# Cross-attention with a state-space tail: two chunk pairs' weighted values issued together in every second step

## The chip, the cores and the metric

The kernel runs on one core of one Trainium2 chip. The metric is the device time of one execution in microseconds (us), the median of several. A core has five engines that each take their own instructions in order and wait for one another through semaphores: TensorE (PE, matrix products into the accumulator memory PSUM; its weight loads are listed apart as PEld), VectorE (DVE), ScalarE (ACT), GpSimd (POOL) and SyncE (SP, which here only issues transfers).

## The reference

The input `x` is 4096 rows of 512, the context 3202 rows of 512. Both are layer-normalized with the same gain and shift, then eight attention heads of 64 go from `x` to the context; the result is projected and added to `x`. A second layer norm, a projection to 64 states, a scan along the 4096 rows (`s = silu(s @ A.T) + u`), and a projection back follow, with two more additions. The part around the change is the attention:

```python
scores = jnp.einsum('bhqd,bhkd->bhqk', q, k) * (1.0 / np.sqrt(HD))
attn = jax.nn.softmax(scores, axis=-1)
out = jnp.einsum('bhqk,bhkd->bhqd', attn, v)
```

Everything is float32. The scan comes last and is done in 16 interleaved chunks.

## The kernel before

**Three stages.** First the context is normalized, keys and values are computed and written to memory, and the first block of queries is made. Then the attention loop runs. Then the last rows are projected and the scan and the output follow. The change lies in the attention loop.

**The tiling of the loop.** The 4096 queries are eight blocks `Q` of 512. A *unit* is one block, one pair of heads `hp` (four of them) and one half of the block (256 queries): 64 units. The 3202 keys are 26 chunks of 123 or 124, taken as 13 pairs (`NDC = 13`), so a unit has 13 *steps* `c = 0..12`, and there are 832 steps. One step handles two heads x two chunks x 256 queries: a tile of 123 x 1024.

**What one step's tile goes through.**

- `scores` (L460): four float32 products on PE (two recorded passes each, so x8) into a PSUM tile `s`; there are two such tiles in turn (`ps_s`, `bufs=2`). They use the array as two row halves of 64. ACT then copies `s` to SBUF as `p` (L470).
- `running` (L481), one step later: DVE takes the running maximum `top` from `s`. The tile `s` is free again only after this and the copy.
- After the 13th step, `maximum`: PE transposes `top` (`tt`, L492), DVE reduces it (`m`, L499), PE spreads the result over the partitions (`mb`, L507). This takes three steps.
- `subtract` (L515): DVE takes `mb` off `p`, 16 steps (13 + `LAG`) after the scores.
- `weights` (L525), one step later: ACT takes the exponential; POOL adds it to `acc` (L534).
- `product` (L543), one further step later: four products on PE (x8) of `p` with the values into `po`, two column halves of 64.
- `finish` after a unit's last product: ACT copies `po` (L586), POOL folds `acc` (L589), PE transposes (`pd`, L595), DVE reduces and inverts (L600, L601), ACT widens (L603), PE transposes (`rb`, L608), DVE multiplies (L614).

**The order is written by hand.** `manual_schedule` keeps the order of the code on each engine. In a step at position `r` of its unit (`r` is the chunk pair whose scores are made) the loop issues: the running maximum of the step before, the exponential of an older one, scores, subtraction, product, then `mb` at r = 2, then *background* work, then `tt` at r = 0. The product lags the scores by 18 = 13 + 5 steps, so at position `r` it is that of chunk pair (r + 8) mod 13, of the unit before or the one before that: pair 8 at r = 0, 9 at r = 1, 12 at r = 4, 0 at r = 5.

**Background** is a queue of generators, advanced a little in each step: `finish` of every unit, `project` of a finished block (four tiles: the output projection `pa`, L628, on PE, then a layer norm and the state projection `pu`), and `queries` for the next block (transposes `tp_x` of four tiles, then four batches `pq`, L172). In a standard block the first and last units and most of the units of the last block have only `finish`; three units carry `project`, two carry the query transposes, one carries the four `pq` batches.

**Buffers.** `sp_` holds the tiles `p`: 20 of them. `ps_o` holds one `po`. K and V tiles of a head pair are 13 each (`kp`), loaded four steps ahead by SP.

Of the kernel before, what the change touches and what calls it, by code (L numbers as in the profile page):

```python
# [22 lines left out]
NDC = NCH // 2  # L23
# [5 lines left out]
LAG = 3  # L29
# [7 lines left out]
def keys(c):  # L37
    return CK if c < GC else CK - 1


def key0(c):
    return c * (CK - 1) + min(c, GC)
# [3 lines left out]
def xattn_ssm_kernel(  # L46
# [100 lines left out]
    def queries(Q):  # L147

        xns = []
        for half in range(2):  # L150
            xn = xnp.tile([P, NC, QU], F32, tag="xn", name=f"xn_{Q}_{half}")
            xns.append(xn)
            for t in range(NT // 2):
                r = Q * QB + half * QU + t * P
                xt = xp_.tile([P, H], F32, tag="x", name=f"x_{r}", bufs=3)
                nc.sync.dma_start(xt, x[r : r + P, :])
                yield False
                scaled = normalize(xt, P, f"x{r}", later=True)
                yield False
                yield False  # L160
                xh = scaled()
                yield False
                tp = transposes(ps_m, "m", xh, P, f"x{r}")
                yield True
                nc.scalar.copy(xn[:, :, t * P : (t + 1) * P], tp)
                yield False
                yield False
        for hp in range(NC):
            pq = ps_m.tile([P, 512], F32, tag="m", name=f"pq_{Q}_{hp}")
            for half in range(2):  # L170
                for i in range(NC):
                    nc.tensor.matmul(  # L172
                        pq[:, half * QU : (half + 1) * QU],
                        wq[:, i, hp * P : (hp + 1) * P],
                        xns[half][:, i, :],
                        start=(i == 0),
                        stop=(i == NC - 1),
                    )
            yield True
            t = qp.tile([P, QB], F32, tag="q", name=f"q_{Q}_{hp}")  # L180
            nc.scalar.activation(
                t, pq, AF.Identity, bias=bias[:, hp : hp + 1], scale=HD**-0.5
            )
            qt[Q, hp] = t
            yield False
# [179 lines left out]
    with tc.manual_schedule():  # L365
# [17 lines left out]
        for c in range(NCH):  # L383
# [28 lines left out]
            for hp in range(NC):  # L412
# [13 lines left out]
                for b in range(g * GC, c + 1, 2):  # L426
                    m, k = 2 * keys(b), key0(b) - key0(g * GC)
# [6 lines left out]
    lctx = ExitStack()  # L434
# [11 lines left out]
    op = actx.enter_context(tc.tile_pool(name="op", bufs=6))  # L446
    small = actx.enter_context(tc.tile_pool(name="small", bufs=2))
    kp = lctx.enter_context(tc.tile_pool(name="kp", bufs=NDC))
    sp_ = lctx.enter_context(tc.tile_pool(name="sp_", bufs=NDC + LAG + 4))

    o_t = {}

# [19 lines left out]
    def running(w, c):  # L472

        n, s = keys(2 * c), w["ps"]
        if c == 0:
            w["top"] = w["s"][0]
            return
        before = w["top"]
        if c == 1:
            w["top"] = accp.tile([CK, 2, 2, QU], F32, tag="top", name=f"top_{w['name']}")  # L480
        nc.vector.tensor_tensor(w["top"][:n], s[:n], before[:n], ALU.max)  # L481
# [31 lines left out]
    def subtract(w, c):  # L513
        n, t = keys(2 * c), w["s"][c]
        nc.vector.tensor_tensor(  # L515
            t[:n],
            t[:n],
            w["mb"][:n].unsqueeze(2).to_broadcast([n, 2, 2, QU]),
            ALU.subtract,
        )  # L520

    def weights(w, c):

        n, t = keys(2 * c), w["s"][c]
        nc.scalar.activation(t[:n], t[:n], AF.Exp)  # L525
        if w["last"] and c in PE_SUMS:
            return
        before = w.get("acc")
        if before is None:
            w["acc"] = t  # L530
            return
        if c == 1:
            w["acc"] = accp.tile([CK, 2, 2, QU], F32, tag="acc", name=f"acc_{w['name']}")
        nc.gpsimd.tensor_tensor(w["acc"][:n], t[:n], before[:n], ALU.add)  # L534

    def product(w, c):

        n, t = keys(2 * c), w["s"].pop(c)
        if c == 0:
            w["po"] = ps_o.tile([P, 2, QU], F32, tag="o", name=f"po_{w['name']}")  # L540
        for b in range(2):
            for a in range(2):
                nc.tensor.matmul(  # L543
                    w["po"][a * HD : (a + 1) * HD, 0, :],
                    vts[(*w["at"][:2], c)][:n, b, a * HD : (a + 1) * HD],
                    t[:n, a, b, :],
                    start=(c == 0 and b == 0),
                    stop=(c == NDC - 1 and b == 1),
                )
        if w["last"] and c in PE_SUMS:  # L550

            if c == PE_SUMS[0]:
                w["pd"] = ps_m.tile([P, 512], F32, tag="m", name=f"pd_{w['name']}")
            sums(w["pd"], t, n, c == PE_SUMS[0], False)

    def sums(pd, t, n, start, stop):
        for b in range(2):
            for a in range(2):
                nc.tensor.matmul(
                    pd[a * HD : (a + 1) * HD, :QU],  # L560
                    ones[:n],
                    t[:n, a, b, :],
                    start=(start and b == 0),
                    stop=(stop and b == 1),
                )
# [109 lines left out]
    def load_k(i, c):  # L675

        Q, hp, half = units[i]
        if half == 0:
            t = kp.tile([P, 2 * CK], F32, tag="k", name=f"k_{Q}_{hp}_{c}")
            n = 2 * keys(2 * c)  # L680
            nc.sync.dma_start(t[:, :n], kd[hp, c, :, :n])
            kts[Q, hp, c] = t

    def load_v(i, c):
        Q, hp, half = units[i]
        if half == 0:
            t = kp.tile([CK, 2, P], F32, tag="v", name=f"v_{Q}_{hp}_{c}")
            n = keys(2 * c)
            nc.sync.dma_start(t[:n], vd[hp, c, :n])
            vts[Q, hp, c] = t  # L690
# [9 lines left out]
    def at(k):  # L700

        if 0 <= k < len(steps):
            return ws[steps[k][0]], steps[k][1]
# [15 lines left out]
    with tc.manual_schedule():  # L719
        for g in range(AHEAD):  # L720
            load_k(*steps[g])
        for g in range(len(steps) + NDC + LAG + 2):
            b = g - NDC - LAG
            if g + AHEAD < len(steps):
                load_k(*steps[g + AHEAD])
            if 0 <= b + AHEAD < len(steps):
                load_v(*steps[b + AHEAD])
            if g < len(steps):
                i, c = steps[g]
                Q, hp, half = units[i]  # L730
                if c == 0:
                    ws[i] = dict(
                        name=f"{Q}_{hp}_{half}", at=units[i], s={}, last=i == len(units) - 1,
                        q=qt[Q, hp][:, half * QU : (half + 1) * QU],
                    )
                    if (hp, half) == (1, 1) and Q + 1 < NQB:
                        rest.append(queries(Q + 1))
            now, prev, sub, exp, mul = at(g), at(g - 1), at(b), at(b - 1), at(b - 2)

            ends = {k: at(g - k)[0] for k in (1, 2, 3) if at(g - k) and at(g - k)[1] == NDC - 1}  # L740
            if 3 in ends and sub:
                subtract(*sub)
            if prev:
                running(*prev)
            if exp:
                weights(*exp)
            if now:
                scores(*now)
            if 3 not in ends and sub:
                subtract(*sub)  # L750
            if 2 in ends:
                next(ends[2]["max"])
            if mul:
                product(*mul)
                if mul[0]["last"] and mul[1] == NDC - 1:
                    finish_last(mul[0])
                elif mul[1] == NDC - 1:
                    first.append(finish(mul[0]))
                    if mul[0]["at"][1:] == (NC - 1, 1):
                        rest.insert(0, project(mul[0]["at"][0]))  # L760
            if 3 in ends:
                next(ends[3]["max"], None)
            background(more=1 not in ends)
            if 1 in ends:
                ends[1]["max"] = maximum(ends[1])
                next(ends[1]["max"])
        while first or rest:
            background()
# [200 lines left out]
```

## Time and profile before

| | before |
|---|---|
| median of 3 runs | 2682.13 us (2678.46 to 2682.83) |
| the profiled execution's own time | 2679.33 us |
| its span in the profile | 2677.4 us |
| PE, DVE, ACT, POOL busy, share of the span | 94%, 80%, 69%, 77% |
| mean granted TensorE clock | 0.977 of full |
| attention loop, first scores to last product | 304.8 to about 2538 us |

The profile is of one execution. Its page gives busy shares, the chain of work that ended last, groups of instructions by source line, and issues of transfers; the trace behind it answers for single stretches of time. In the listings of instructions in order of time the columns are the start in us, the duration in us, the engine, the line, the operation, the tile written <- the tiles read, their shapes, the count, and in brackets idle time before it and what ended it. The end of a product on PE is modelled, so the distance from one block's start to the next is the better measure. The table by stretches lists, for each engine, busy us and (x instructions), then the granted clock.

### The profile page before, as it was taken

How to read it: one execution, taken by the hardware profiler on the slowest of the kernel's cores; microseconds unless marked ns; L12 is line 12 of the kernel's file. 1: busy time of each engine (PE TensorE's matmuls, PEld its weight loads, DVE VectorE, ACT ScalarE, POOL GpSimd, SP SyncE). 2: the span in 40 equal slices, each digit the busy share in tenths (PEclk: the TensorE clock that was granted, in tenths of full speed). 3: DMA queues.
4: the chain of work that ended last, by engine and by line, in shares of the span. 5: the costliest groups of instructions: out<-in, count | busy, mean ns of one | idle time of the engine just before them, and what ended most of it. 6: DMA issues, size and time to landing. Idle time of an engine off the chain costs nothing.

```text
span 2677.4 us, 44182 instructions
## 1 busy us (share of the span) xinstructions
PE 2507.3 (94%) x16588; PEld 1424.4 (53%) x16588; DVE 2146.1 (80%) x2321; ACT 1836.0 (69%) x2085; POOL 2065.1 (77%) x1170
## 2 busy tenths in 40 slices
PE   7788799999999999999999999999999999999957
PEld 3333555555565556555555556555555565555533
DVE  2121298899979998999989897999799979999825
ACT  2122387787878787877878787878687878788610
POOL 1111099899979998999979897999799979999870
PEclk9889999999999999999999999999999999999976
DMA  4332221112212221122111221212112211221043
GB/s 123 90 92 85 77 67 45 46 57 68 70 41 58 59 75 47 53 67 70 58 50 56 81 60 43 61 52 82 33 55 69 69 42 58 58 65 54 27 147 126
DMA packets 167551, 176.62 MB, mean 66 GB/s; under 512 B 16701, under 2 KB 140645, under 8 KB 167335
## 3 DMA queue, kind: packets, MB, share of 16 engines
q1 hardware_dynamic: 155374, 158.21, 20.0%
q10 hardware_dynamic: 11961, 15.54, 1.9%
q8 instruction: 134, 2.20, 0.3%
q14 instruction: 82, 0.67, 0.1%
HBM read 143.81 MB, written 29.89 MB: 65 GB/s over the span
## 4 chain that ended last, share of the span: by engine, by line
PE 44%; DVE 26%; issue 18%; ACT 8%; POOL 3%; DMA 2%; SPq 0%; ACTq 0%; DVEq 0%; POOLq 0%
DVE top L481 17%; PE s L460 14%; PE po L543 12%; DVE p L515 5%; PE pq L172 4%; ACT p L470 4%; PE pa L628 4%; ACT p L525 2%; PE tt L492 2%; PE py_c L871 1%; DVE rd L600 1%; PE mb L507 1%; PE pu L660 1%; PE pk L415 1%; POOL acc L534 1%
## 5 line engine op out<-in xcount | busy, mean ns | idle before, releaser
L534 POOL TENSOR_TENSOR acc<-p,acc 123x1024 f32<-123x1024 f32 x698 | 1657.0, 2374 | 115.3 <-ACT p L525 73.8
L470 ACT COPY p<-s 123x1024 f32<-123x1024 f32 (+1 forms) x832 | 834.2, 1003 | 274.1 <-PE s L460 263.4
L515 DVE TENSOR_TENSOR p<-p,mb 123x1024 f32<-123x1024 f32 (+1 forms) x832 | 1001.2, 1211 | 0.8 <-PE mb L507 0.8
L460 PE MATMUL s<-q,k 64*123 64x256 f32 (+1 forms) x6656 | 940.0, 401 | 61.0 <-DVE top L481 50.6
L525 ACT ACTIVATE p<-p 123x1024 f32<-123x1024 f32 (+1 forms) x832 | 880.1, 1058 | 143.7 <-DVE p L515 137.1
L481 DVE TENSOR_TENSOR top<-s,top 123x1024 f32<-123x1024 f32 x704 | 856.7, 1217 | 139.4 <-ACT p L470 130.6
L543 PE MATMUL po<-p,v 123*64 123x256 f32 (+1 forms) x6656 | 901.3, 392 | 1.1 <-ACT o L586 0.9
L460 PEld LDWEIGHTS s<-q,k 64*123 64x123 f32 (+1 forms) x6656 | 559.3, 181 | 373.6 <-DVE top L481 172.5
L543 PEld LDWEIGHTS po<-p,v 123*64 123x64 f32 (+1 forms) x6656 | 404.8, 136 | 399.4 <-issue 223.1
L534 POOL TENSOR_TENSOR acc<-p,p 124x1024 f32<-124x1024 f32 x64 | 151.9, 2374 | 152.6 <-ACT p L525 152.3
L115 POOL TENSOR_SCALAR ve_c<-mv_c 123x1 f32<-123x1 f32 (+1 forms) x26 | 6.1, 233 | 187.7 <-DVE mv_c L113 181.6
L111 DVE BATCH_NORM_STATS2 st_c<-cx 123x6 f32<-123x512 f32 (+1 forms) x26 | 18.0, 692 | 151.8 <-DMA cx<-in_ctx_dram 151.8
L628 PE MATMUL pa<-wo,o 128*128 128x512 f32 x256 | 119.5, 611 | 2.3 <-DVE x L637 2.3
L172 PE MATMUL pq<-xn,wq 128*128 128x256 f32 x512 | 117.9, 383 | 0.0
L481 DVE TENSOR_TENSOR top<-s,p 124x1024 f32<-124x1024 f32 x64 | 77.9, 1217 | 40.6 <-DMA k<-kd 39.3
L125 ACT ACTIVATE xh_c<-cx,nmr_c,rstd_c 123x512 f32<-123x512 f32 (+1 forms) x26 | 21.1, 812 | 129.1 <-POOL nmr_c L119 129.1
L172 PEld LDWEIGHTS pq<-xn,wq 128*128 128x128 f32 x512 | 95.0, 190 | 20.7 <-issue 6.3
L415 PE MATMUL pk<-ct,wk 128*128 128x492 f32 (+2 forms) x224 | 99.0, 599 | 3.3 <-ACT ks L423 3.3
L390 PE MATMUL pv<-wv,ct 128*123 128x512 f32 (+1 forms) x208 | 96.3, 607 | 0.0
L589 POOL TENSOR_TENSOR both<-acc 124x512 f32<-124x512 f32 x63 | 80.8, 1283 | 4.9
L499 DVE TENSOR_REDUCE m<-tt 128x2 f32<-128x496 f32 x128 | 79.9, 665 | 0.7 <-PE tt L492 0.7
L628 PEld LDWEIGHTS pa<-wo,o 128*128 128x128 f32 x256 | 46.8, 192 | 62.2 <-issue 56.3
(157 smaller groups left out, 1335.3 us busy)
## 6 DMA issues: line engine op xcount, KB each, us to landing
k<-kd SPq DMA_DIRECT2D x352, 123.0 KB
v<-vd SPq DMA_DIRECT2D x352, 123.0 KB
x<-in_x_dram SPq DMA_DIRECT2D x32, 256.0 KB
xr<-in_x_dram SPq DMA_DIRECT2D x32, 256.0 KB
out_dram<-row_c ACTq DMA_DIRECT2D x32, 256.0 KB
k<-kd SPq DMA_DIRECT2D x64, 124.0 KB
v<-vd SPq DMA_DIRECT2D x64, 124.0 KB
x1d<-x SPq DMA_DIRECT2D x28, 256.0 KB
```

Source lines behind the costliest of these rows:

```text
L172: nc.tensor.matmul(pq[:, half * QU : (half + 1) * QU], wq[:, i, hp * P : (hp + 1) * P], xns[half][:, i, :], start=(i == 0), stop=(i == NC ...
L390: nc.tensor.matmul(pv[:n, :H], ct[:, i, o : o + n], wv[:, i, :], start=(i == 0), stop=(i == NC - 1),)
L415: nc.tensor.matmul(pk[:, :n_g], wk[:, i, hp * P : (hp + 1) * P], ct[:, i, :n_g], start=(i == 0), stop=(i == NC - 1),)
L460: nc.tensor.matmul(s[:n, a, b, :], kts[(*w["at"][:2], c)][r, b * n : (b + 1) * n], q[r], start=True, stop=True,)
L470: nc.scalar.copy(t[:n], s[:n])
L481: nc.vector.tensor_tensor(w["top"][:n], s[:n], before[:n], ALU.max)
L515: nc.vector.tensor_tensor(t[:n], t[:n], w["mb"][:n].unsqueeze(2).to_broadcast([n, 2, 2, QU]), ALU.subtract,)
L525: nc.scalar.activation(t[:n], t[:n], AF.Exp)
L534: nc.gpsimd.tensor_tensor(w["acc"][:n], t[:n], before[:n], ALU.add)
L543: nc.tensor.matmul(w["po"][a * HD : (a + 1) * HD, 0, :], vts[(*w["at"][:2], c)][:n, b, a * HD : (a + 1) * HD], t[:n, a, b, :], start=(c == ...
L589: nc.gpsimd.tensor_tensor(both, acc[:, :, 0, :], acc[:, :, 1, :], ALU.add)
L628: nc.tensor.matmul(pa, o_t[Q, c][:, t * P : (t + 1) * P], wo[:, c, :], start=(c == 0), stop=(c == NC - 1),)
```

## The change

The product of an even chunk pair is no longer issued in its own step. The step of an odd chunk pair issues two products, of the pair before and its own; the 13th chunk pair, which is even, is issued alone in its own step. Scores, subtraction, exponential, sums and background keep their places. Since an even tile `p` is read one step later, the pool `sp_` gets one more buffer, 21.

```diff
-    sp_ = lctx.enter_context(tc.tile_pool(name="sp_", bufs=NDC + LAG + 4))
+    sp_ = lctx.enter_context(tc.tile_pool(name="sp_", bufs=NDC + LAG + 5))
...
             if mul:
-                product(*mul)
+
+                u_, c = mul
+                for k in (c - 1, c) if c % 2 else (c,) if c == NDC - 1 else ():
+                    product(u_, k)
                 if mul[0]["last"] and mul[1] == NDC - 1:
                     finish_last(mul[0])
                 elif mul[1] == NDC - 1:
```

## The prediction

> **What bounds the kernel now.** I began with the page's busy shares and the chain that ended last.
>
> ```profile
> PE 2507.3 (94%) x16588; PEld 1424.4 (53%) x16588; DVE 2146.1 (80%) x2321; ACT 1836.0 (69%) x2085; POOL 2065.1 (77%) x1170
> PE 44%; DVE 26%; issue 18%; ACT 8%; POOL 3%; DMA 2%; SPq 0%; ACTq 0%; DVEq 0%; POOLq 0%
> ```
>
> PE looks like the bound, but both lines are means over different stages. So I cut one block's eight units apart, by their first score copy, and took the busy time of each engine in each: two with query transposes, one with `pq`, two with only `finish` ("plain"), three with `project`.
>
> ```profile
> 979.60:1012.30 32.70, 31.23 (x240) 17.84 (x236) 32.20 (x36) 27.87 (x33) 31.17 (x20) 1.00 0.11 36
> ...
> 1045.00:1090.10 45.10, 44.33 (x294) 28.79 (x294) 31.00 (x31) 28.55 (x34) 30.48 (x15) 1.00 0.07 21
> 1090.10:1121.00 30.90, 29.80 (x228) 16.86 (x228) 30.67 (x31) 26.12 (x28) 29.72 (x14) 1.00 0.28 78
> ...
> 1186.00:1224.90 38.90, 38.90 (x264) 21.45 (x261) 34.88 (x39) 28.18 (x32) 34.89 (x22) 1.00 0.18 53
> ```
>
> After the length come PE, PEld, DVE, ACT, POOL. The plain unit (third line) has DVE busy 30.67 of 30.90 us: DVE sets its length, PE does not. PE is the bound only with `project` (38.90 of 38.90) and in the `pq` unit. Of the 64 units 20 are plain, 14 have query transposes, 21 `project`, 7 `pq`, 2 are the lead-in.
>
> Next, the plain unit in order of time: PE from its position 0 to 3, DVE and ACT beside it.
>
> ```profile
> 1090.02 1.08 PE L543 MATMUL po<-p,v 123*64 123x256 f32 x8
> 1091.22 1.07 PE L492 MATMUL tt<-ident,top 124*128 124x124 f32 x8
> 1092.22 1.13 PE L460 MATMUL s<-q,k 64*124 64x256 f32 x8
> 1093.28 1.08 PE L543 MATMUL po<-p,v 123*64 123x256 f32 x8
> 1094.30 1.13 PE L460 MATMUL s<-q,k 64*123 64x256 f32 x8
> 1095.36 1.08 PE L543 MATMUL po<-p,v 123*64 123x256 f32 x8
> 1096.37 0.65 PE L507 MATMUL mb<-ident,m 128*124 128x128 f32 x4
> 1096.95 1.13 PE L460 MATMUL s<-q,k 64*123 64x256 f32 x8
> ```
>
> ```profile
> 1089.95 1.22 DVE L481 TENSOR_TENSOR top<-s,top 123x1024 f32<-123x1024 f32 x1
> ...
> 1095.64 1.22 DVE L481 TENSOR_TENSOR top<-s,p 124x1024 f32<-124x1024 f32 x1
> 1096.96 1.23 DVE L481 TENSOR_TENSOR top<-s,top 123x1024 f32<-123x1024 f32 x1
> ```
>
> ```profile
> 1095.53 1.02 ACT L470 COPY p<-s 123x1024 f32<-123x1024 f32 x1
> ...
> 1098.18 1.01 ACT L470 COPY p<-s 123x1024 f32<-123x1024 f32 x1 [0.69 <-PE s L460]
> ```
>
> Three readings. A block `s` followed by `po` takes 1.06 us (1092.22 to 1093.28), `po` followed by anything else 1.01. From the start of `s` to its copy is 1.23 us (1094.30 to 1095.53, 1096.95 to 1098.18), and the maximum can start 1.04 after the copy starts (elsewhere, 1054.05 to 1055.09): 2.27 in all. So the maximum over scores 2, issued at position 3 and started at 1096.96, could have started at 1094.30 + 2.27 = 1096.57: PE has 0.39 us in hand there, on a DVE that never rests.
>
> Last, blocks of one kind in a row: scores in the lead-in, products and sums (the same array split) in the tail.
>
> ```profile
> 329.53 2.00 PE L460 MATMUL s<-q,k 64*124 64x256 f32 x16
> 331.45 0.65 PE L507 MATMUL mb<-ident,m 128*124 128x128 f32 x4
> ```
>
> ```profile
> 2528.80 1.90 PE L543 MATMUL po<-p,v 123*64 123x256 f32 x16
> 2530.53 1.03 PE L559 MATMUL pd<-p,ones 123*64 123x256 f32 x8
> ```
>
> Two `s` and a switch take 1.92, so `s` after `s` costs 0.86; two `po` take 1.73, 0.87 each. A switch out of `s` thus costs 0.19-0.20, out of `po` 0.14-0.15.
>
> **What the Trainium skill says.** "TensorEngine Tiling (Array Packing)", Key Properties: changing the tiling mode, not just the tile, drains the array; agreed, with the two prices above. "TensorE: Matmul & The Clock Gate", The mechanism: products start and end in program order, so a second product delays the next scores; agreed, PE's blocks run in the order of the code. "PSUM — Partial Sum Buffer", PSUM bank collisions: the compiler adds a dependency between ACT and DVE on one bank, even for two reads; agreed, the maximum starts 1.04 us after the copy of the same `s`, never beside it. Same page, Engine vs sequencer instructions: DVE and ACT are strict first-in first-out, so a late maximum delays every subtraction behind it.
>
> **The change part by part.**
>
> *Array switches.* Where nothing else stands between, a pair of steps goes from four switches to two: 0.34 us of PE saved. Where the step without a product holds a `tt`, `mb` or other background, only 0.15. A plain unit has four pairs of the first sort and two of the second: 4 x 0.34 + 2 x 0.15 = 1.66 us. DVE covers PE there, so this buys nothing by itself.
>
> *Placement.* Pairs fall at r = 1 (chunk pairs 8, 9), 3, 6, 8, 10, 12; chunk pair 12 alone at 4; none at 0, 2, 5, 7, 9, 11.
>
> *Position 0, plain unit.* Before, product 8 ran from 1090.02 to 1091.03, and `tt` waited until 1091.22 for the maximum of 1089.95. Afterwards the pair at r = 12 pushes the scores of r = 0 from 1088.96 to 1089.64; `tt` could go at 1090.70, but still waits until 1091.22. Scores 1 start at 1092.22 as before. Product 8, formerly free, is now in front.
>
> *Position 1.* 1092.22 + 1.06 + 0.87 + 1.01 = 1095.16 for scores 2, against 1094.30: 0.86 late. Maximum at 1095.16 + 2.27 = 1097.43 instead of 1096.96: DVE stalls 0.47. Behind it wait the first subtraction, then the exponential on ACT, POOL's sum, the next maximum.
>
> *Position 2.* No product; `mb` at 1096.22, 0.15 early; scores 3 wait for the maximum that ends at 1096.86, start 1096.91.
>
> *Position 3.* Products 10, 11: scores 4 at 1096.91 + 2.94 = 1099.85 against 1099.03. Their maximum at 1102.12, while DVE (1101.50 before, + 0.47) is free at 1101.97: 0.15 more. The copy of `po` shifts with product 12 and pushes ACT some 0.05. Sum 0.65 us a plain unit, 20 of them: 13.0.
>
> *Later positions.* After a pair the next scores come 2.94 after the last, where DVE's pace is 2.26: 0.68 late. The scores of 1086.70 could be copied at 1087.93 and are at 1088.77, because an exponential stands before: 0.84 in hand covers it. With the cover gone it would be up to 0.68 at four places, 2.7 us a unit.
>
> *Query-transpose units.* DVE has a layer-norm statistic (0.69 + 0.18) just before that maximum; in the unit of 979.6 scores 2 at 984.12 feed a maximum at 987.11, 0.72 in hand; `tt` does not wait there, so scores 2 come only 0.57 late. At position 4 0.18 late on ACT remains: 0.2 x 14 = 2.8.
>
> *`pq` units.* PE runs without pause from scores 1 to scores 5: before 1047.09 to 1070.37. `tt` again waits for the maximum (1046.09), so product 8 moves into the stretch (+1.01) and two `po`-after-`po` save 0.14 each: +0.7 x 7 = 4.9.
>
> *`project` units.* I followed PE and DVE in the same way through 1152-1250, where PE bounds. Example, the unit of 1186: `tt` waits, so scores 1 start at 1188.64 (1188.66 before), then 1.06 + 0.87 + 1.01 + 3.65 for `pa`: scores 2 at 1195.23 against 1194.36, their maximum 0.86 later. Positions 2, 5, 7 and 9 have no product, but `mb`, `tp_y`, `pu`, `pa`: each loses 1.01 of PE work and gives it back, less 0.15 or 0.34, at the next position. DVE's lag falls to 0.1 by scores 5; the `pa` at position 9, with no product ahead of it, brings scores 10 at 1217.09 instead of 1217.56, and the maximum is 0.48 ahead; the next pair takes that back. It ends near +0.2: 7 blocks, 1.4.
>
> *Nothing:* the lead-in has no products. In the tail without scores the order on PE is the same. The later release of an even `p` is met by the 21st buffer (two steps between product and reuse, as before); V tiles are reloaded nine steps after their last product, eight afterwards; no DMA moves. No step adds an instruction.
>
> Sum 13.0 + 2.8 + 4.9 + 1.4 = 22 us. On the profiled execution's 2679.3 that is 2701; the median lies 2.8 above it, so **2704 us**, 0.8% slower.
>
> **Rivals.**
>
> 1. *PE's time counts everywhere* (the chain's 44% and 18% issue speak for it): 1.66 x 62 = 103 us saved, 2579. Against: DVE rests 0.23 us in a plain unit. 3 in 100.
> 2. *The other side, milder:* the 0.39 us in hand for scores 2 is really above 0.86 (were the copy able to start sooner after its scores, say), so nothing stalls in plain units, and in the 21 `project` units PE's saving of 1.09 us each (five pairs at 0.15, one at 0.34) is kept: -23 at best, so 2659 to 2682. It decides from the point where scores 2 are late by less than what is in hand. Against: 1.23 and 1.04 recur wherever the copy waits for PE. 5 in 100.
> 3. *Hidden:* the stalls for scores 2 and 4 are repaid by the gains with `project`: within 5 us. 7 in 100.
> 4. *The later positions are not covered:* 0.68 at one to two of the four pairs beyond position 4, on some 34 units: 22 + 23 to 46, so 2727-2750. For: `pd` (0.57) and `rb` (0.37) stand behind pairs at r = 6 and 8. Against: DVE's own reduction for them (0.67 + 0.18) falls there too. 17 in 100.
>
> The forecast itself has 68 in 100; its own range is 2694 to 2716: from 0.45 us a plain unit and nothing with `project` to 0.9 a plain unit and 0.4 on the others.
>
> **How the numbers follow.** 0.2% (5.4 us) is about what a measurement of this kernel can tell from no change. Faster: rivals 1 and 2, 0.07 (part of 2 falls within). Same: 0.08. Slower: 0.85. For 8 in 10 the range reaches from 2688, the lower part of the forecast, to 2728, the near edge of rival 4.
>
> **What would show it.** Right: in plain units, about 31.6 us instead of 30.9; the running maximum L481 waits on the copy about 0.47 for scores 2 in every plain unit, so its idle time (139.4 us now) grows by some 15-25 us; `po` x16 blocks of 1.9 us; PE busy down by up to 100 us; DVE busy unchanged. Wrong: plain units still 30.9 (the margin was larger), or shorter; stalls of L481 at positions 7, 9 or 11 (rival 4); a longer tail; or ACT or PE waiting for `p` buffers or V tiles.

## The result and the profile after

The changed kernel takes 2707.68 us (median of 6 runs, 2699.59 to 2713.03) against 2680.57 us for the kernel before (6 runs, 2675.43 to 2685.05): a ratio of 1.0097, 95% interval 1.0073 to 1.0121, so some 27 us slower. The profiled execution took 2711.29 us, its span is 2709.4 us.

From the page, the busy shares and the groups of the maximum and of the product:

```profile
PE 2461.1 (91%) x16588; PEld 1464.8 (54%) x16588; DVE 2148.3 (79%) x2321; ACT 1837.1 (68%) x2085; POOL 2066.3 (76%) x1170
...
L481 DVE TENSOR_TENSOR top<-s,top 123x1024 f32<-123x1024 f32 x704 | 856.3, 1216 | 169.6 <-ACT p L470 163.2
...
L543 PE MATMUL po<-p,v 123*64 123x256 f32 (+1 forms) x6656 | 822.2, 388 | 0.5 <-ACT o L586 0.5
```

TensorE did get its saving: it is 46 us less busy (2507.3 before), L543 alone 79 us less (901.3 before). DVE is as busy as before, 2148.3 against 2146.1, and idles 30 us more ahead of the running maximum L481 (139.4 before). The kernel got longer by about what DVE waits more.

The same units as before, cut at their first score copy (length, PE, PEld, DVE, ACT, POOL, then the granted clock): the second with query transposes, the one with `pq`, a plain one, the second with `project`.

```profile
1026.93:1060.81 33.88, 31.74 (x234) 19.00 (x235) 32.21 (x35) 28.55 (x33) 31.81 (x20) 0.95 0.28 83
1060.81:1106.46 45.65, 43.07 (x290) 29.32 (x290) 30.85 (x30) 28.41 (x33) 28.99 (x14) 1.00 0.06 19
1106.46:1138.02 31.56, 28.88 (x226) 17.43 (x226) 30.78 (x31) 26.20 (x30) 29.79 (x14) 1.00 0.29 80
...
1203.67:1242.36 38.69, 37.39 (x254) 21.66 (x254) 34.54 (x38) 28.03 (x32) 34.64 (x22) 1.00 0.19 54
```

The plain unit is 31.56 us instead of 30.93, with PE 0.9 us less busy. And the first line shows something else: a mean granted clock of 0.95 in the middle of the loop, where the loop ran at 1.00 throughout before.

PE through positions 0 to 4 of that plain unit, in order of time, and below it DVE's maxima over scores 1, 2 and 4 (parts left out) and ACT's copy of scores 2:

```profile
1106.65 1.07 PE L492 MATMUL tt<-ident,top 124*128 124x124 f32 x8 [0.46 <-DVE top L481]
1107.65 1.13 PE L460 MATMUL s<-q,k 64*124 64x256 f32 x8
1108.71 1.95 PE L543 MATMUL po<-p,v 123*64 123x256 f32 x16
1110.59 1.13 PE L460 MATMUL s<-q,k 64*123 64x256 f32 x8
1111.65 0.65 PE L507 MATMUL mb<-ident,m 128*124 128x128 f32 x4
1112.34 1.13 PE L460 MATMUL s<-q,k 64*123 64x256 f32 x8
1113.40 1.95 PE L543 MATMUL po<-p,v 123*64 123x256 f32 x16
1115.28 1.13 PE L460 MATMUL s<-q,k 64*123 64x256 f32 x8
```

```profile
1111.07 1.22 DVE L481 TENSOR_TENSOR top<-s,p 124x1024 f32<-124x1024 f32 x1
1112.86 1.22 DVE L481 TENSOR_TENSOR top<-s,top 123x1024 f32<-123x1024 f32 x1 [0.58 <-ACT p L470]
...
1116.27 1.21 DVE L515 TENSOR_TENSOR p<-p,mb 124x1024 f32<-124x1024 f32 x1
1117.55 1.22 DVE L481 TENSOR_TENSOR top<-s,top 123x1024 f32<-123x1024 f32 x1
```

```profile
1111.82 1.01 ACT L470 COPY p<-s 123x1024 f32<-123x1024 f32 x1 [0.97 <-PE s L460]
```

PE stands still for 0.46 us until DVE lets `tt` go. Then come scores 1 (1107.65) and both products, and scores 2 start only 2.94 us after scores 1; their copy starts 1.23 us after that, and their maximum 1.04 us after the copy. DVE stood still for 0.58 us, of which 0.1 is the gap between these two maxima before. The maximum over scores 4 starts 1.28 us after the subtraction ahead of it, where it was 1.13 before (1100.37 to 1101.50): 0.15 more. The two stalls together are the 0.63 us of the unit.

By kind of unit, the change of length against the profiled execution of before, taken from the start of every 13th score copy:

| units | each | sum, us |
|---|---|---|
| 19 plain (the 20th is the last of all and runs into the tail) | 18 of +0.62 to 0.64, one 0.74 | +12.0 |
| 14 with query transposes | nine +0.16 to 0.24, five +1.15 to 1.38 | +8.2 |
| 7 with `pq` | +0.56 to 0.69 | +4.4 |
| 21 with `project` | -0.16 to +0.15 | +0.7 |
| 2 at the start | +0.39, 0 | +0.4 |
| loop, to the start of its last unit | | +25.7 |
| the rest of the span, in this pair of executions | | +6.3 |

Hardly any of the last row can be put down to the change: the start of the loop and its tail move by several us from one execution to the next (the first score copy stands between 303 and 313 us in the traces of this study, with the same code ahead of it).

### The profile page after: what moved, and what is told of

Its sections match the earlier page's. It is cut to its first block, busy times and chain, and to the rows that moved or that the text cites. A ratio compares the mean times of both kernels' runs of the same rounds, so it can differ in the third digit from the quotient of the medians.

```text
span 2709.4 us, 44139 instructions
## 1 busy us (share of the span) xinstructions
PE 2461.1 (91%) x16588; PEld 1464.8 (54%) x16588; DVE 2148.3 (79%) x2321; ACT 1837.1 (68%) x2085; POOL 2066.3 (76%) x1170
## 4 chain that ended last, share of the span: by engine, by line
PE 45%; DVE 23%; issue 17%; ACT 10%; POOL 3%; DMA 1%; SPq 0%; ACTq 0%; DVEq 0%; POOLq 0%
DVE top L481 16%; PE s L460 15%; PE po L543 13%; ACT p L470 6%; PE pq L172 4%; PE pa L628 4%; DVE p L515 4%; ACT p L525 2%; PE tt L492 2%; PE py_c L874 1%; PE mb L507 1%; PE pk L415 1%; PE pu L660 1%; POOL acc L534 1%; PE pd L595 1%
## 5 line engine op out<-in xcount | busy, mean ns | idle before, releaser
L481 DVE TENSOR_TENSOR top<-s,top 123x1024 f32<-123x1024 f32 x704 | 856.3, 1216 | 169.6 <-ACT p L470 163.2
L543 PE MATMUL po<-p,v 123*64 123x256 f32 (+1 forms) x6656 | 822.2, 388 | 0.5 <-ACT o L586 0.5
L543 PEld LDWEIGHTS po<-p,v 123*64 123x64 f32 (+1 forms) x6656 | 440.3, 137 | 328.4 <-issue 117.7
L481 DVE TENSOR_TENSOR top<-s,p 124x1024 f32<-124x1024 f32 x64 | 77.7, 1214 | 41.0 <-DMA k<-kd 39.7
L492 PE MATMUL tt<-ident,top 124*128 124x124 f32 x512 | 68.2, 276 | 34.8 <-DVE top L481 34.3
L492 PEld LDWEIGHTS tt<-ident,top 124*128 124x128 f32 x512 | 53.6, 141 | 60.7 <-DVE top L481 60.7
```

The costliest lines, as they stand in the source:

```text
L492: nc.tensor.transpose(tp[:, a, b, :], w["top"][:, a, b, t * P : (t + 1) * P], ident[:CK, :CK],)
L543: nc.tensor.matmul(w["po"][a * HD : (a + 1) * HD, 0, :], vts[(*w["at"][:2], c)][:n, b, a * HD : (a + 1) * HD], t[:n, a, b, :], start=(c == ...
```

## The experiments

**Theories.** A, the prediction's: scores 2 and 4 come late, because at positions 1 and 3 a second product stands ahead of them, where less is in hand than it takes. B: every doubled product costs DVE alike, wherever it is. C: the longer ring of `p` buffers costs it. Unit lengths are compared with the profiled execution of before, as above; where a kernel ran only once, they carry the argument, and its time does not.

The diffs are shortened. In each the set holds the chunk pairs whose product is put off to the next step; the changed kernel's is (0, 2, 4, 6, 8, 10). `SET` is a short form of this text: the kernels have the tuple written out. All of them keep the 21st buffer.

```diff
+                if c - 1 in SET:
+                    product(u_, c - 1)
+                if c not in SET:
+                    product(u_, c)
```

**The buffer alone.**

```diff
+                SET = ()        # and sp_ bufs=NDC + LAG + 5
```

> The kernel before with the 21st buffer alone, every product in its own step. Theory A (scores 2 and 4 come late because a second product stands ahead of them, at positions where there are under 0.4 us in hand): a plain unit is 30.93 us as before, the time within 5 us of before. Rival C (the longer ring of p buffers, or where it lies in memory, costs something): a plain unit above 31.1, up to 31.56 as in the changed kernel.

Measured: plain units 30.93 (two of them 0.27 longer), all others within 0.01 us but the two of the lead-in (+0.97 and 0.32); one run of 2685.45 us against a median of 2683.93. C is out: the buffer does not lengthen the plain units.

**Two pairs of the six.**

```diff
+                SET = (8, 10)
```

> Only the chunk pairs 8 with 9 and 10 with 11 are issued together; 0 to 7 and 12 alone in their own steps. Theory A: the whole price is here, a plain unit takes 31.5 to 31.6 us, with a stall of DVE of about 0.5 before the maximum over scores 2 and one of about 0.15 before that over scores 4. Rival B (each doubled product costs DVE alike, 0.63 / 6 = 0.105 a pair): 30.93 + 0.21 = 31.14.

```profile
1105.96:1137.52 31.56, 29.60 (x226) 17.06 (x226) 30.78 (x31) 26.21 (x29) 29.76 (x14) 1.00 0.28 76
```

The plain unit, in the same columns, is 31.56: all of the price with a third of the pairs, +0.63 or 0.64 in each of 19. B is out. And this kernel's loop is 7 us longer than the changed one's (33.1 us over before against 25.7; 2718.59 us in its one run), since project units now lose 0.4 to 0.8 each: the four pairs taken back were worth some 12 us there.

**The other four pairs.**

```diff
+                SET = (0, 2, 4, 6)
```

> Chunk pairs 0 with 1, 2 with 3, 4 with 5, 6 with 7 are issued together; 8 to 12 alone. Theory A: a plain unit is back at 30.9 to 31.0 though four of six pairs are left (PE saves 4 x 0.34 us there and nothing comes of it); the pq unit is back near 45.1; project units are 0.1 to 0.8 shorter than before, so the whole is 2 to 15 us under the kernel before. Rival B: 30.93 + 0.42 = 31.35 in a plain unit, the whole some 10 to 20 us above before.

Measured: ratio 1.0049 (1.0035 to 1.0063), some 12 us slower where I expected 2 to 15 us faster. Plain units cost +0.48 where A as I stated it wanted 0, and `pq` units +0.46 to 0.69 where it wanted 0 too; project units were 0.23 to 0.61 shorter, as expected, and five units with query transposes had a window of half clock (below). By itself this run fits B (+0.42 a plain unit, 10 to 20 us in all) better than A. PE at positions 12 to 1 of a plain unit shows another reason:

```profile
1090.89 1.95 PE L543 MATMUL po<-p,v 123*64 123x256 f32 x16
1092.77 1.13 PE L460 MATMUL s<-q,k 64*124 64x256 f32 x8
1093.83 1.08 PE L543 MATMUL po<-p,v 123*64 123x256 f32 x8
1094.84 1.07 PE L492 MATMUL tt<-ident,top 124*128 124x124 f32 x8
1095.84 1.13 PE L460 MATMUL s<-q,k 64*124 64x256 f32 x8
```

The pair 6 and 7 (first line) holds up scores 0, then product 8, and `tt` starts at 1094.84 without waiting: 0.5 us behind the maximum it needs, which ended at 1094.30. From there scores 1, 2 and 3 are late, and the maxima over scores 2 and 3 stall DVE 0.20 and 0.30. In the changed kernel that delay vanished in `tt`'s wait. So the two covers hang together; my expectation had carried the wait over to a kernel that no longer has it. The prediction's own figures would have given it: scores 0 at 1089.64, then 1.06 and, with product 8 in its place again, 1.01 put `tt` at 1091.71, 0.49 after the 1091.22 of before.

**Three pairs**, to test that reading.

```diff
+                SET = (0, 2, 4)
```

> Chunk pairs 0 with 1, 2 with 3, 4 with 5 are issued together in every unit; 6 to 12 alone. If the 0.48 us that plain units still lost with four pairs came from the pair 6 with 7, which holds up scores 0, product 8 and so tt, a plain unit is now 30.93 to 31.0. If it came from the pairs 0 to 5 themselves, it stays near 31.4. Project units 0.4 to 0.6 shorter, pq as before. In query-transpose units TensorE may still fall to half clock for a window, 1.1 to 1.2 us each, since position 9 has no product. The whole 0 to 12 us under the kernel before.

Measured: plain units within 0.03 us of before, but for two of +0.27 and one of +0.10: the 0.48 was the pair 6 and 7, and B fails again, which wanted some 0.3 for three pairs. Project units 0.26 to 0.73 shorter, 10.3 us in all. `pq` units +0.34 to 0.42, not expected and not settled. Yet the ratio is 1.0002 (0.9987 to 1.0017): seven of the 14 units with query transposes took 1.40 to 1.56 us more, each with a window of half clock. More on it below.

**One pair fewer, and slower.**

```diff
+                SET = (0, 2, 4, 6, 8)
```

> The changed kernel with chunk pairs 10 and 11 back in their own steps. Theory A, worked out as in the prediction: scores 2 are 0.86 late as before, and product 10 at position 2 now keeps scores 3 late by 0.86 too (1097.81 against 1096.95), where the changed kernel had won that time back: stalls of 0.47 and 0.38, so a plain unit gets longer, 31.7 to 31.8 us, although one pair fewer is doubled. Rival B: shorter, 31.45.

DVE at positions 3 and 4 of a plain unit:

```profile
1117.02 1.23 DVE L481 TENSOR_TENSOR top<-s,top 123x1024 f32<-123x1024 f32 x1 [0.58 <-ACT p L470]
...
1119.68 1.22 DVE L481 TENSOR_TENSOR top<-s,top 123x1024 f32<-123x1024 f32 x1 [0.30 <-ACT p L470]
```

Plain units +0.85 or 0.86 (16 of 19) where the changed kernel has +0.63, though only five pairs are doubled: the maxima over scores 2 and, now, 3 stall. This tells A from B most sharply: the sign and the size were worked out from the trace of before.

**As many pairs, one position earlier.**

```diff
+                SET = (1, 3, 5, 7, 9, 11)
```

> As many doubled products as in the changed kernel, but of an odd chunk pair with the next even one (1 with 2 up to 11 with 12, 0 alone), so they fall at positions 0, 2, 4, 7, 9, 11, and 1 and 3 have none. Theory A, worked out from the trace of before as in the prediction: scores 2 are no longer late behind products, but tt comes 0.7 later and ACT's order holds the copy back: a plain unit 31.2 to 31.3 (0.14 and 0.18 of stall), a pq unit about 45.3, the whole 3 to 12 us above before. Rival B, which sees only the number of pairs: a plain unit 31.56 again, the whole 22 to 30 us above before.

Measured: plain units +0.32 or 0.33 (16 of 19), `pq` units +0.31, as A has it. The whole was a miss, 1.0090 (1.0071 to 1.0109), some 23 us against an expected 3 to 12: I had worked out only these two kinds. That the whole falls into B's 22 to 30 us says little for B, since the plain units, at 31.25, are not the 31.56 it wanted. Project units cost +8.2 us and those with query transposes +9.0 (two with half clock, +2.0 and 2.2); where in them was not followed up.

**Pairs only where PE is the bound.**

```diff
+                j = units.index(u_["at"])
+                SET = (0, 2, 4, 6) if j >= 8 and j % 8 < 3 else ()
```

> Chunk pairs 0 with 1 to 6 with 7 are issued together only for the products that fall into the 21 project units, where PE runs without pause; everywhere else each product has its own step, as before. Theory A: project units are 0.4 to 0.7 us shorter each (those of the run that left 8 to 12 alone were 0.23, 0.49 and 0.61 shorter, the first with 0.5 of entry stall in it), plain, query-transpose and pq units unchanged: 10 to 14 us under the kernel before, and TensorE stays at full clock in the loop. Rival B: each pair costs DVE something even here, so nothing or a loss.

A plain and a project unit, columns as above:

```profile
1087.70:1118.60 30.90, 29.81 (x228) 16.89 (x226) 30.67 (x31) 26.14 (x30) 29.73 (x14) 1.00 0.27 77
1183.10:1221.40 38.30, 38.18 (x262) 21.77 (x258) 34.55 (x38) 27.98 (x32) 34.59 (x22) 1.00 0.18 55
```

The ratio is 0.9938 (0.9915 to 0.9960), median 2662.95 us, faster than both kernels. Project units are 0.72, 0.5 and 0.61 us shorter, 12.9 us in all, the rest is within 0.03 us of before but for two plain units of +0.27 (the same two as with the buffer alone) and one of the lead-in (+0.07), and the clock stays full in the loop. A saving on PE that buys nothing in a plain unit is nearly all kept where PE has no rest (38.90 of 38.90 us busy before): PE is 13.8 us less busy in the 21 units, and they are 12.9 us shorter.

**The half clock.** In the changed kernel five windows of 3.4 us inside the loop, behind its lead-in, ran at half clock, all in units with query transposes. Five such windows stand in the trace with pairs 0 to 7, seven each in those with pairs 0 to 5 and 0 to 9, two in that with odd pairs, all in these units; with the buffer alone, with pairs 8 to 11 and with `project` alone there are none, as before. Here is PE around one of the changed kernel's, and the busy time in two stretches of 3.4 us; the last line is from before, around position 9 of such a unit:

```profile
1047.56 1.13 PE L460 MATMUL s<-q,k 64*123 64x256 f32 x8
1050.42 1.13 PE L460 MATMUL s<-q,k 64*123 64x256 f32 x8 [1.73 <-DVE top L481]
1051.48 3.22 PE L543 MATMUL po<-p,v 123*64 123x256 f32 x16
```

```profile
1048.60:1052.00 3.40, 1.68 (x16) 1.05 (x16) 3.30 (x6) 2.23 (x3) 3.13 (x5) 1.00 0.14 37
1052.00:1055.40 3.40, 3.40 (x18) 1.80 (x16) 3.40 (x4) 3.17 (x4) 3.32 (x2) 0.50 0.15 42
```

```profile
1003.30:1006.70 3.40, 2.26 (x18) 1.28 (x20) 3.40 (x5) 2.23 (x3) 3.13 (x5) 1.00 0.18 59
```

At position 9 there is no product any more. DVE has a layer-norm statistic to do (0.69 and 0.18 us) ahead of the maximum that frees the tile for the next scores, and PE waits 1.73 us, where with the product it waited 0.98. The window is half busy (1.68 of 3.40), the next one is granted 0.50, and the next pair of products takes 3.22 us instead of 1.95.

Taking the pair 4 and 5 back puts work at that position:

```diff
+                SET = (0, 2, 6, 8, 10)
```

> The changed kernel with chunk pairs 4 and 5 back in their own steps. It is for the half clock: in the changed kernel's trace TensorE ran five windows of 3.4 us at half clock inside the loop, each after a window in which it was busy for half the time only, at position 9 of a query-transpose unit, which had no product. If that rest is the cause, none is left here in the loop and all 14 of these units are 0.1 to 0.3 us over before, none 1.2; plain units stay at 31.56; project units lose some 0.2. If the half clock is chance, or comes from other places, it is seen here as well.

Measured: 1.0077 (1.0056 to 1.0097); no half clock in any of the 14 units, +0.07 to 0.23 each. Plain units stay at 31.56, and project units are 0.16 longer on average than in the changed kernel. "None in the loop" was too much: one window fell into a plain unit (that unit +2.10), again after one of the least busy windows, 54% by the modelled ends.

The direct test adds useless work at position 9 of those 14 units to the kernel with three pairs, and the diff is against that kernel:

```diff
+                if c == 4 and (j in (2, 3) or (8 < j < 55 and j % 8 in (3, 4))):
...
+                            nc.tensor.matmul(
+                                idle[a_ * HD : (a_ + 1) * HD, :QU],
+                                vts[(*u_["at"][:2], c)][:n_, b_, a_ * HD : (a_ + 1) * HD],
+                                t_[:n_, a_, b_, :],
...
                 if c - 1 in (0, 2, 4):
```

> The kernel of the run pairs_0_to_5 with useless work added: in the 14 query-transpose units, at position 9, which has no product there, PE makes the product of chunk pair 4 once more into a tile that nobody reads (8 recorded passes, 0.87 us a unit, 12 us of added PE work in all). If TensorE falls to half clock because it was busy for too little of one 3.4 us window there, no half-clock window is left in the loop, all 14 units are within 0.3 us of before, where seven of them took 1.4 to 1.55 more, and the whole is 4 to 11 us shorter than pairs_0_to_5 for all the added work: 2672 to 2679, 0.996 to 0.999 of before. If the half clock has another cause (or none that the program sets), windows of it are seen in the loop as before and the added work makes the units longer.

The same unit, first of the kernel with three pairs, then with the added work:

```profile
1858.47:1892.57 34.10, 32.05 (x236) 18.74 (x234) 32.29 (x35) 28.39 (x33) 31.80 (x19) 0.95 0.28 80
```

```profile
1856.78:1889.46 32.68, 31.43 (x246) 18.49 (x244) 32.11 (x36) 28.27 (x33) 31.35 (x20) 1.00 0.29 83
```

No half clock is left in those units or anywhere in the steady loop, and all 14 are within 0.03 us of before. The kernel takes 2675.22 us where that without the work took 2683.37 (medians of 22 and 16 runs; ratios to before 0.9977, 0.9965 to 0.9988, and 1.0002, 0.9987 to 1.0017): about 8 us faster for 12 us more work.

## Why the prediction was right

*DVE is the bound, PE's saving buys nothing in plain units:* right. PE's plain unit lost 0.9 us of work and the unit grew; the kernel with pairs 0 to 5 takes 0.6 us of PE work from a plain unit on average and leaves its length alone. The saving itself was put too high, at 1.66 us a plain unit where the busy time fell by 1.0 on average (0.92 in the one shown), and at 103 us in all where it fell by 46; as DVE covers PE there, the forecast of plain units did not hang on it.

*Positions 0 to 3:* right to a few hundredths. From the start of scores 1, scores 2 were to start 2.94 us later and started 2.94 later; scores 3 4.69, measured 4.69; scores 4 7.63, measured 7.63. The unit was to grow by 0.65 us and grew by 0.63. The kernel with pairs 8 to 11 alone has the whole of it, so that it comes from these two pairs is shown, not only argued.

*Query-transpose units:* 0.2 each was right in nine (0.16 to 0.24). In the other five the prediction missed a term, the half clock, 5.4 us in the profiled execution. It put PE's added rest at nothing and did not name it. With those five at 0.2 the loop would have grown by 20.3 us against the 22 of the sum.

*`pq` units:* +0.7 forecast, +0.68 or 0.69 measured in the four with no half clock just before them, +0.56 in the other three.

*`project` units:* +0.2 a block forecast, +0.1 measured; the gain of the positions without a product and the stall of position 1 do cancel.

*What was to be seen:* `po` blocks of 1.95 us, plain units 31.6: right. The wait of L481 grew by 30, not 15 to 25, us; PE busy fell by 46, which "up to 100" allows, but it is less than half of that.

*The rivals:* PE's time does not count everywhere (the first), the 0.39 us in hand for scores 2 was not really above 0.86, since DVE stalled there by the 0.48 worked out (the second), and project units repay nothing (the third). The fourth, stalls at later positions, did not appear; but the kernel with pairs 0 to 7 shows that with the two early pairs gone the pair at position 12 does cost, 0.48. In the changed kernel `tt`'s wait covers it, as the prediction has it at position 0; the kernel with pairs 0 to 7 no longer has that wait.

*The size:* the forecast of 2704 lies 4 us under the measured median, and this nearness is in part luck. In the profiled pair the loop grew by 25.7 us: the half clock, which the sum of 22 did not have, added 5.4, and the terms for plain, `pq` and `project` units, too large by some 2 together, took part of that back. There is a trace of one execution of the changed kernel only, so how much half clock the others had is not shown.

## What to carry to other kernels

Work put off on an engine that is not the bound still delays what is queued behind it: find the place where the bounding engine takes its next input, and measure how much is in hand there, position by position; the mean busy share says nothing of it. A saving on an engine is worth its price only in the stretches where that engine has no rest, so apply it there alone. Two covers can hang on one another: after undoing one part, work the rest out afresh.

## What the hardware showed that I had not expected

TensorE fell to half clock for 3.4 us after one window of that length in which it was busy for about half the time; in the case shown the rest was a single one of 1.73 us, and in the other cases the longest rest was 1.13 to 2.04 us. Each such window cost some 1.0 to 1.8 us of its unit. Filling that rest with useless products removed the windows and made the kernel with three pairs faster.

In the traces of all the kernels here the granted clock changes only on a grid of 3.413 us. Cut the loop along that grid, from its third unit to its last scores, and take PE's modelled busy time in each window: 31 windows had 40 to 50%, and 24 of them were followed by half clock; 17 had over 51 and under 54%, and 3 were; of those with more none was, and the least busy window of the kernel before had 62%. The same rest of 1.72 or 1.73 us lay whole in one window 27 times, and half clock followed 20 times; 21 times the grid cut it in two, and half clock never followed. So in these traces the busy share of a window on the grid tells more than the length of the rest, and where the grid falls decides in part which of the 14 units is hit. Why 7 of the 31 windows were not followed stays open.
